# Products with h in pairs of 64 stationary columns on both column halves of the array, for two heads of one batch

## Chip, core and metric

The kernel runs on one core of a Trainium2 chip. Times are device microseconds of an execution of the whole program. TensorE multiplies: it loads a stationary tile (up to 128 rows by 128 columns) and streams a moving tile through it, with the result in PSUM. VectorE (DVE), ScalarE (ACT) and GpSimd (POOL) do the elementwise work, and SyncE (SP) issues most of the DMAs. All data are fp32.

## The reference, cut to what matters

There are two graph layers on 16 batches of 1024 nodes with 128 features, each followed by a residual sum and a layer norm. Layer 1 is the one that the change touches. Its input `X` is layer 0's output, its `A` is the adjacency, and it has four heads:

```
h      = einsum('bnf,hfd->hbnd', X, conv_w) + conv_b
scores = einsum('hbni,hij,hbmj->hbnm', h, attn_w, h)
Ah     = tanh(A * scores)
hh     = relu(einsum('hbnm,hbmd->hbnd', Ah, h))
out    = layernorm(X + relu(relu(mean over heads of hh) + X))
```

Layer 0 is an attention over the same adjacency with a masked softmax, three gates and a tanh. Of it only its place beside layer 1 matters here.

## The kernel before

Layer 1 of a batch is 32 steps: 4 heads (`hd`) by 8 blocks of 128 nodes (`m`). A step, `layer1_step(b, hd, m)`, does four things.

1. TensorE multiplies block `m` of the transposed input `x1T` with the head's `uT` (the input times the head's folded weights), in two halves `q` of 512 columns, into PSUM tiles `sc` (L704).
2. DVE multiplies each half with the adjacency into the SBUF tile `s`, 128 x 1024 (L705).
3. ACT takes the tanh of `s` in place (L706).
4. `back` multiplies `s` with the head's 128 columns of `h1` of block `m`, and adds that to the head's accumulator `acc`, 128 x 1024 in two PSUM banks (L710). The stationary operand is `h1[:, ts(hd, D)]`, 128 x 128; the moving one is a half of `s`, 128 x 512. So a step has two such products, one for each `q`, with the features of the head as output partitions and the nodes as columns. Over the 8 blocks they add up in PSUM.

After a head's eighth block, `add_head` adds the ReLU of each half of `acc` to the tile `sum` on DVE (L726 for head 0, L728 for the others). The accumulator has one buffer under its tag, so the next head's first product with h waits until both of these have read it.

The products with h are not issued in their own step. `push` puts each `back` into the queue `pending`, and with `DELAY = 2` the products of a step are issued two steps later, behind that step's score products. TensorE so has 2 steps for DVE and ACT to finish `s`.

The order of the instructions is written out by hand. Between the steps of batch b, the tables `BETWEEN` and `AHEAD` place pieces of layer 0 of batch b+1 (its products with the attention at L462, masks, softmax, gates) and of batch b+2 (its score products at L354). `head_uT` (L238) makes the next head's `uT` at a head's fifth block. There is a semaphore wait only where another engine or a DMA is to be waited for.

Another kind of TensorE product is used below for its times: in the opening, `weigh_bias` multiplies a stationary tile of only 3 rows, `rows_x` (L157), between the products at L153 and L158, whose stationary tiles are 128 x 128.

Of the kernel before, what the change touches and what calls it, by code (L numbers as in the profile page):

```python
# [24 lines left out]
def two_layer_adjacency_kernel(  # L25
# [19 lines left out]
    nc = tc.nc  # L45
    B, N, D = x.shape
    H = conv_w.shape[0]
    assert D == P and N % 512 == 0
    NB = N // P
# [144 lines left out]
    def push(back):  # L194
        pending.append(back)
        if len(pending) > DELAY:
            pending.popleft()()
# [489 lines left out]
    def layer1_step(b, hd, m):  # L687
        x1T, h1, uT = x1T_t[b], h1_t[b, m], u_t[b, hd]
        adj = adj_t[b, m]
        if m == 0:  # L690
            acc1_t[b, hd] = ps_acc.tile([P, N], F32, tag="acc1", name=f"acc1_{b}_{hd}")
        acc = acc1_t[b, hd]


        last = (b, hd) == (B - 1, H - 1)
        if last:
            if m == 0:
                kept.append(sb.tile([P, NB, N], F32, tag="R", name="kept", bufs=1))
            s = kept[0][:, m, :]
        else:  # L700
            s = sb.tile([P, N], F32, tag="s1", name=f"s1_{b}_{hd}_{m}", bufs=4)
        for q in range(NH):
            ps = ps_sc.tile([P, 512], F32, tag="sc", name=f"sc1_{b}_{hd}_{m}_{q}")
            nc.tensor.matmul(ps, x1T[:, ts(m, P)], uT[:, ts(q, 512)], start=True, stop=True)  # L704
            nc.vector.tensor_mul(s[:, ts(q, 512)], ps, adj[:, ts(q, 512)])  # L705
        nc.scalar.activation(s, s, AF.Tanh)  # L706

        def back(halves=range(NH)):
            for q in halves:
                nc.tensor.matmul(  # L710
                    acc[:, ts(q, 512)], h1[:, ts(hd, D)], s[:, ts(q, 512)],
                    start=(m == 0), stop=(m == NB - 1),
                )
            if m == NB - 1:
                if hd == 0:
                    sum_t[b] = sb.tile([P, N], F32, tag="sum", name=f"sum_{b}", bufs=1)
                for q in halves:
                    add_head(b, hd, acc[:, ts(q, 512)], q * 512)

        push(partial(back, [0]) if last else back)  # L720

    def add_head(b, hd, a, at):

        o = sum_t[b][:, at : at + a.shape[1]]
        if hd == 0:
            nc.vector.tensor_scalar_max(o, a, 0.0)  # L726
        else:
            nc.vector.scalar_tensor_tensor(o, a, 0.0, o, op0=ALU.max, op1=ALU.add)  # L728
# [142 lines left out]
    for b in range(B):  # L871
        plan = BETWEEN if b else {**BETWEEN, **FIRST}
        after = layer0(b + 2) if b + 2 < B else {}
        for step in range(H * NB):
            hd, m = divmod(step, NB)
# [81 lines left out]
```

## Time and profile before

| | |
|---|---|
| runs, device us | 2409.5, 2409.74, 2414.6; median 2409.74 |
| span of the profiled execution, first to last instruction | 2407.4 us |
| TensorE matmuls and weight loads in the profile | 5983 and 5983 |
| granted TensorE clock, mean | 0.999 of full speed |
| head 1 of batch 8, products with h | about 1299.7 to 1338.7 us of the span |
| head 2 of batch 8, products with h | about 1338.7 to 1372.8 us of the span |

The profiled execution has no time of its own besides its span; the median of the runs is 2.3 us above the span, which is what lies before the first and behind the last instruction.

The profile numbers the lines of the kernel before. "PE" is a matmul, "PEld" a weight load, which can run under a matmul. In a group's row stand the line, engine and operation, the tiles written and read, the tile of the array with its shape, and the number of instructions; then the busy time in us and the mean length of one in ns; then the engine's idle time ahead of them and what ended it. A matmul's recorded length runs from its start to its modelled end, so the lengths of two that follow each other overlap. The starts say what each costs.

### The profile page before, as it was taken

The page shows a single profiled execution, that of the slowest core. Times are in us where ns is not written, and L with a number is a line of the kernel's source. Part 1 is how long each engine was busy: PE and PEld are TensorE (multiplying, and loading weights), DVE is VectorE, ACT ScalarE, POOL GpSimd, SP SyncE. Part 2 cuts the span into 40 slices and gives each one's busy share as a digit, 9 for nine tenths or more (in the row PEclk, how much of TensorE's full clock was granted, in tenths as well). Part 3 has the DMA queues.
Part 4 walks back from the last instruction along what each step waited for, and adds up shares of the span by engine and source line. Part 5 has one row for each costly group of instructions (what it writes and reads, how often), then busy time and mean ns, then how long its engine had stood idle before and what let it go on. Part 6 is the DMA issues. An engine that isn't in the chain of part 4 may idle for free.

```text
span 2407.4 us, 20166 instructions
## 1 busy us (share of the span) xinstructions
PE 2398.8 (100%) x5983; PEld 1095.6 (46%) x5983; DVE 1551.3 (64%) x3262; ACT 1063.5 (44%) x1503; POOL 608.9 (25%) x389
## 2 busy tenths in 40 slices
PE   9999999999999999999999999999999999999999
PEld 5444444444444444444444444444444444444444
DVE  7666666766667656666666666667666576666555
ACT  6545344453444534445444454444444344443333
POOL 2214131241312313133131231313214132141000
PEclk9999999999999999999999999999999999999999
DMA  5334151442414324243242422425234252341010
GB/s 192 72 78 123 46 130 42 97 106 50 126 47 104 94 60 115 53 111 82 63 113 62 115 69 70 110 56 123 62 78 108 51 131 53 80 115 34 18 27 10
DMA packets 474194, 196.98 MB, mean 82 GB/s; under 512 B 414948, under 2 KB 440291, under 8 KB 474084
## 3 DMA queue, kind: packets, MB, share of 16 engines
q1 hardware_dynamic: 455501, 129.03, 23.0%
q0 software_dynamic: 18288, 66.59, 9.3%
q8 instruction: 48, 0.79, 0.1%
q14 instruction: 63, 0.51, 0.1%
q10 hardware_dynamic: 294, 0.07, 0.0%
HBM read 136.12 MB, written 59.51 MB: 81 GB/s over the span
## 4 chain that ended last, share of the span: by engine, by line
PE 99%; DVE 1%; ACT 0%; issue 0%; POOLq 0%; DVEq 0%
PE sc L704 36%; PE acc L710 36%; PE acc L462 9%; PE sc L354 5%; PE pR L675 5%; PE pT_u L238 5%; PE pR_h L335 1%; PE pT_q L238 1%; PE acc_other L462 0%; PE idle L136 0%; DVE R L418 0%; DVE s L705 0%; PE pt L496 0%; DVE st L214 0%; PE turn L371 0%
## 5 line engine op out<-in xcount | busy, mean ns | idle before, releaser
L705 DVE TENSOR_TENSOR s<-sc,adj 128x512 f32<-128x512 f32 x1008 | 685.1, 688 | 713.9 <-PE sc L704 692.7
L706 ACT ACTIVATE s<-s 128x1024 f32<-128x1024 f32 x504 | 533.1, 1058 | 1056.9 <-DVE s L705 897.7
L704 PE MATMUL sc<-uT,x1T 128*128 128x512 f32 x2048 | 962.8, 592 | 0.2
L710 PE MATMUL acc<-s,h 128*128 128x512 f32 x2016 | 947.3, 592 | 0.0
L710 PEld LDWEIGHTS acc<-s,h 128*128 128x128 f32 x2016 | 380.5, 190 | 484.7 <-issue 476.7
L704 PEld LDWEIGHTS sc<-uT,x1T 128*128 128x128 f32 x2048 | 386.7, 190 | 470.2 <-issue 403.5
L401 POOL TENSOR_SCALAR edge<-adj 128x1024 uint8<-128x1024 f32 x120 | 332.8, 2773 | 315.3 <-DVE top_None L418 312.9
L218 POOL TENSOR_TENSOR rs<-rs,mhalf 128x8 f32<-128x8 f32 (+3 forms) x35 | 54.2, 1549 | 881.0 <-DVE rs L217 880.9
L462 PE MATMUL acc<-R,hz 128*128 128x512 f32 x492 | 231.6, 592 | 0.2 <-ACT hz L448 0.2
L430 ACT ACTIVATE R<-R,nmax 128x1024 f32<-128x1024 f32 x126 | 144.6, 1147 | 81.0 <-DVE nmax L426 73.3
L418 DVE CUSTOM_DVE_ANT_0 R<-R,edge 128x1024 f32<-128x1024 f32 x126 | 152.8, 1213 | 0.5 <-ACT hz L448 0.5
L451 DVE TENSOR_TENSOR R<-R,adj 128x1024 f32<-128x1024 f32 (+1 forms) x127 | 152.0, 1197 | 0.0
L462 PEld LDWEIGHTS acc<-R,hz 128*128 128x128 f32 x492 | 93.1, 190 | 115.7 <-issue 111.4
L354 PE MATMUL sc<-xT,qT 128*128 128x512 f32 (+3 forms) x384 | 144.9, 486 | 0.0
L360 ACT ACTIVATE R<-sc,h 128x512 f32<-128x512 f32 (+1 forms) x192 | 111.1, 580 | 52.3 <-PE sc L354 46.8
L543 POOL TENSOR_TENSOR x1T<-hp,wu_b 128x1024 f32<-128x1024 f32 x45 | 106.4, 2363 | 103.8 <-DVE hws L549 63.6
L238 PE MATMUL pT_u<-x1T,ms 128*128 128x512 f32 x256 | 120.6, 593 | 0.0
L675 PE MATMUL pR<-cw,x1T 128*128 128x512 f32 x256 | 117.6, 598 | 0.0
L354 PEld LDWEIGHTS sc<-xT,qT 128*128 128x128 f32 x384 | 69.9, 190 | 70.0 <-issue 60.6
L302 POOL DMA_DIRECT2D adj<-in_adjT_dram x112 | 66.1, 590 | 91.8 <-DVE s L705 91.8
L728 DVE SCALAR_TENSOR_TENSOR sum<-acc,sum 128x512 f32<-128x512 f32 x95 | 61.2, 686 | 41.7 <-PE acc L710 41.7
L678 ACT COPY h<-pR 128x512 f32<-128x512 f32 x128 | 72.4, 593 | 28.2 <-PE pR L675 26.4
(163 smaller groups left out, 1151.5 us busy)
## 6 DMA issues: line engine op xcount, KB each, us to landing
adj<-in_adjT_dram POOLq DMA_DIRECT2D x112, 512.0 KB, 4.1
xT<-in_xT_dram SPq DMA_DIRECT2D x16, 512.0 KB, 4.7
adj<-in_adjT_dram SPq DMA_DIRECT2D x16, 512.0 KB, 8.8
x<-in_x_dram SPq DMA_DIRECT2D x16, 512.0 KB, 5.5
dram_hp<-turn_hp SPq DMA_DIRECT2D x15, 512.0 KB, 2.6
hp<-dram_hp SPq DMA_DIRECT2D x60, 128.0 KB, 3.1
dram_x<-turn_x SPq DMA_DIRECT2D x15, 512.0 KB, 2.9
x1T<-dram_x SPq DMA_DIRECT2D x60, 128.0 KB, 5.5
```

Source lines behind the costliest of these rows:

```text
L238: nc.tensor.matmul(ps, w, src[:, ts(q, 512)], start=True, stop=True)
L354: nc.tensor.matmul(ps[:, : at - lo], t["qT"][:, ts(j, P)], t["xT"][:, lo:at], start=True, stop=True)
L401: engine.tensor_scalar(m, adj_t[b, j], 0.0, None, ALU.is_gt)
L418: nc.vector.tensor_tensor_reduce(to[:, ks], s[:, ks], t["edge", j][:, ks], 1.0, nmax, ALU.mult, ALU.max, top)
L430: nc.scalar.activation(row(j), row(j), AF.Exp, bias=t["nmax", j], accum_out=t["z", j])
L451: nc.vector.tensor_mul(s[:, ks], s[:, ks], adj[:, ks])
L462: nc.tensor.matmul(t["acc"][q], t["hz", j], row(j)[:, ts(q, BH), :], start=(j == 0), stop=(j == NB - 1),)
L675: nc.tensor.matmul(ps, x1T_t[b][:, ts(k, P)], cw.rearrange("p h d -> p (h d)"), start=True, stop=True)
L704: nc.tensor.matmul(ps, x1T[:, ts(m, P)], uT[:, ts(q, 512)], start=True, stop=True)
L705: nc.vector.tensor_mul(s[:, ts(q, 512)], ps, adj[:, ts(q, 512)])
L706: nc.scalar.activation(s, s, AF.Tanh)
L710: nc.tensor.matmul(acc[:, ts(q, 512)], h1[:, ts(hd, D)], s[:, ts(q, 512)], start=(m == 0), stop=(m == NB - 1),)
```

## The change

In batch 8 (`B // 2`), heads 1 and 2, `back` issues four products of 64 stationary columns where it issued two of 128. `c` is the half of the head's 128 columns and `q` the half of the moving columns. Output features 0 to 63 go to PSUM partitions 0 to 63, and features 64 to 127 to partitions 64 to 127, so the first are placed on the left column half of the array and the second on the right one, as tiles of 128 rows by 64 columns. The order is in two pairs: first (`c` 0, `q` 0) with (`c` 1, `q` 1), then (`c` 0, `q` 1) with (`c` 1, `q` 0). A pair uses both column halves, with different moving data and different PSUM banks. The accumulated values are the same as before. All other batches and heads, and everything that isn't TensorE, keep their instructions.

```diff
         def back(halves=range(NH)):
-            for q in halves:
+            if b == B // 2 and hd in (1, 2):
+                for pair in (((0, 0), (1, 1)), ((0, 1), (1, 0))):
+                    for c, q in pair:
+                        nc.tensor.matmul(
+                            acc[ts(c, 64), ts(q, 512)],
+                            h1[:, hd * D + c * 64 : hd * D + (c + 1) * 64], s[:, ts(q, 512)],
+                            start=(m == 0), stop=(m == NB - 1),
+                        )
+                halves_done = ()
+            else:
+                halves_done = halves
+            for q in halves_done:
                 nc.tensor.matmul(
                     acc[:, ts(q, 512)], h1[:, ts(hd, D)], s[:, ts(q, 512)],
                     start=(m == 0), stop=(m == NB - 1),
                 )
```

The product in the new branch is at L712 of the changed kernel, the old one at L721, and the additions of `add_head` at L737 and L739.

## The prediction

> **What bounds the kernel now.** I read the page's busy times first, then the chain that ended last, then the costliest groups, and last the timeline of a product with h. The page's first part and its chain:
>
> ```profile
> PE 2398.8 (100%) x5983; PEld 1095.6 (46%) x5983; DVE 1551.3 (64%) x3262; ACT 1063.5 (44%) x1503; POOL 608.9 (25%) x389
> ```
>
> ```profile
> PE 99%; DVE 1%; ACT 0%; issue 0%; POOLq 0%; DVEq 0%
> PE sc L704 36%; PE acc L710 36%; PE acc L462 9%; PE sc L354 5%; PE pR L675 5%; PE pT_u L238 5%; PE pR_h L335 1%; PE pT_q L238 1%; PE acc_other L462 0%; PE idle L136 0%; DVE R L418 0%; DVE s L705 0%; PE pt L496 0%; DVE st L214 0%; PE turn L371 0%
> ```
>
> TensorE is the whole chain. No other engine is busy for more than 64% of the span, so whatever the change adds on TensorE goes to the end in full, and whatever it moves elsewhere is hidden. The line that changes is L710, 36% of the chain:
>
> ```profile
> L704 PE MATMUL sc<-uT,x1T 128*128 128x512 f32 x2048 | 962.8, 592 | 0.2
> L710 PE MATMUL acc<-s,h 128*128 128x512 f32 x2016 | 947.3, 592 | 0.0
> L710 PEld LDWEIGHTS acc<-s,h 128*128 128x128 f32 x2016 | 380.5, 190 | 484.7 <-issue 476.7
> ```
>
> The program has 1,016 products at L710 (504 steps of two, and the last head's 8 of one); the profile has 2,016 + 16 matmuls. So one fp32 product is two passes, each with a weight load of its own. Next the timeline at 1277 us (columns: start, length, engine, line):
>
> ```profile
> 1276.97 0.19 PEld L710 LDWEIGHTS acc<-s,h 128*128 128x128 f32 x1 [0.24 <-ACT uT L240]
> ...
> 1277.40 1.88 PE L710 MATMUL acc<-s,h 128*128 128x512 f32 x4
> 1277.40 0.19 PEld L710 LDWEIGHTS acc<-s,h 128*128 128x128 f32 x1 [0.24 <-issue]
> ...
> 1277.83 0.19 PEld L710 LDWEIGHTS acc<-s,h 128*128 128x128 f32 x1 [0.24 <-issue]
> ...
> 1278.26 0.19 PEld L710 LDWEIGHTS acc<-s,h 128*128 128x128 f32 x1 [0.24 <-issue]
> ...
> 1278.69 0.19 PEld L462 LDWEIGHTS acc<-R,hz 128*128 128x128 f32 x1 [0.24 <-issue]
> ...
> 1279.12 1.88 PE L462 MATMUL acc<-R,hz 128*128 128x512 f32 x4
> ```
>
> Passes start 0.429 us apart ((1279.12 - 1277.40) / 4 = 0.43), although each lasts 0.592: the last 0.163 us is a tail under the next pass. Every load starts at the start of the pass before its own and is over 0.24 us before it is needed. Loads are free today; a step's products cost 4 x 0.429 = 1.72 us.
>
> **What the Trainium skill says.** "TensorEngine Tiling (Array Packing)", Key Properties: tiles can load and multiply in parallel, but changing the tiling mode drains the engine. The trace has one such place, L157, whose stationary tile has 3 rows, among full-array products:
>
> ```profile
> 7.49 0.25 PE L153 MATMUL p_c<-wb_col,s_ww 128*128 128x1 f32 x1
> ...
> 7.67 0.18 PEld L157 LDWEIGHTS p_x<-ident,rows_x 3*128 3x128 f32 x1
> ...
> 7.78 0.18 PEld L157 LDWEIGHTS p_x<-ident,rows_x 3*128 3x128 f32 x1
> ...
> 7.80 0.25 PE L157 MATMUL p_x<-ident,rows_x 3*128 3x3 f32 x1
> ...
> 7.98 0.19 PEld L158 LDWEIGHTS p_x<-wb_col,a_sym 128*128 128x128 f32 x1
> ```
>
> It agrees: at both changes of form the load is not early. It starts 0.18 us after the matmul before it (7.49 to 7.67, 7.80 to 7.98), which streamed 1 and 3 columns, so nearly all of that is the tail. The next load follows 0.11 us later (7.67 to 7.78), so a load of 128 columns holds the array 0.11 us. "TensorE: Matmul & The Clock Gate", LDWEIGHTS, says that a load's time goes with its columns; for 64 I estimate half of 0.11, 0.05 us. The same page, The mechanism, says that matmuls start and end strictly in program order, and that a load overlaps a running matmul only in other rows; the trace contradicts the latter, since all L710 loads run under matmuls on the same rows. Measured speedup vs the span model gives 2.38 times for three column tiles: column tiles do run together there. No trace here has column tiles, in fp32 or otherwise.
>
> **The change part by part.** Batch 8, heads 1 and 2: 16 steps of 512. In each, two products of 128 stationary columns become four of 64, so 4 passes become 8, of 512 moving columns each. DVE, ACT, POOL and the DMA queues keep their instructions and order. I cost a step against 1.72 us.
>
> 1. Passes. If nothing overlaps: 8 x 0.429, +1.72 us. If the pairs are perfect: 4 x 0.429, +0. The order decides between them. One product's two passes use the same half of the array and come one after the other: A first, A second, B first, B second. With starts in program order, B's first pass can join A's second, but A's first finds no partner, and B's second finds one only in the next pair's first. A step of four products is then five slots, not four: first pass alone, three shared slots, last pass alone. +0.43 us.
> 2. Loads inside the chain. A load goes out when the pass before it starts, so the load for each joining pass is exposed: three times 0.05, +0.15 us. Bounds: 0 if it is pulled ahead, 3 x 0.19 = 0.57 if a whole load is waited for.
> 3. Changes of form. Every paired step lies between full-array products, so there are two per step. Going in, tail 0.18 and load 0.05; coming back, tail 0.18 and load 0.11: 0.52 us. Bounds: 0 if columns need no drain, 2 x (0.163 + 0.19) = 0.71 with whole loads.
> 4. Waits. At the ends of heads 1 and 2 the additions on DVE (L728, moved to L739) wait for the last product of the step. In the trace the first addition at 1371.27 starts after both halves' products, not after its own half's, so the pair order, which finishes both halves late, delays nothing. The next head's first product needs these additions done: they end at 1372.55 and it starts at 1372.78. The 0.23 us of slack grows by the change of form ahead of the score products between. That product also waits for the engine's own earlier matmuls, which ended over a microsecond before. Cost 0; if the cover went, 0.2 us at two places.
>
> A step: 0.43 + 0.15 + 0.52 = 1.10 us. Sixteen: 17.6 us, all on the path, since TensorE waits for nothing in these heads (39.00 of 39.00 us and 34.10 of 34.10 us busy). The span of the profile is 2407.4 us, the median of the runs 2409.7; the sum goes on the median: 2427.4 us.
>
> **The rivals.**
>
> *The halves don't run together in fp32.* Everything is in series: 1.72 + 0.52 = 2.24 us a step, 35.8 us, 2445.5. If loads too were exposed at the 7 changes of tile inside a step (7 x 0.05 x 16 = 5.6), 2451. For it: no row of the profile shows two matmuls streaming at once, and each fp32 pass already takes 0.429 us for 512 columns, so it may need paths that a second tile would want. Against it: the skill's measurement, though it names no fp32.
>
> *Pairs in lockstep.* Both halves take first passes together, then second passes: four slots, with one exposed load of 0.05 in each pair. 0.10 + 0.52 = 0.62 us a step, 9.9 us, 2419.7. It would need B to overtake A's second pass, against program order.
>
> *Not slower.* A pass over half the columns is shorter than 0.429 us. At half, 0.214, five slots are 1.07, and with loads 0.15 and changes of form 0.52 the step is 1.74 against 1.72: 0.4 us in all, 2410. In lockstep with four such slots it is 0.86 + 0.62 = 1.48, -3.8 us, 2406. It decides once five slots fall to 0.21 us each. Against it: passes in the profile cost by moving columns (0.59 for 512, 0.28 for 132), and the change moves no fewer per pass.
>
> **How the numbers follow.** Chain of five slots 0.47 (2419 to 2434, with item 2 or item 3 at its bounds), series 0.36 (2437 with free changes of form, 2451 with exposed loads), lockstep 0.10, not slower 0.07. About what a measurement of this kernel can tell is 0.2%, 4.8 us. Lockstep and the two ahead of it are slower by more than that; of the last 0.07, 0.05 lands within it and 0.02 below. Faster 0.02, same 0.05, slower 0.93. The prediction is the chain's 2427.5 us; the range leaves out no loss and half of the lockstep below, and the worst of the series above: 2415 to 2450.
>
> **What would show it.** In the changed profile the paired matmuls are 128 passes with a 128*64 form. In the chain case B's first pass starts about 0.05 us after A's second, and so on in close twos; in series all eight starts are 0.43 apart. Each paired step is preceded and followed by a load that starts about 0.6 us after the last full pass's start, not with it. Other engines' busy times stay. The forecast is wrong if eight starts are evenly spaced, if no load is late at the change of form, or if steps outside the 16 move.

## The result, and the profile after

The changed kernel takes 2414.82 us (median of 18 runs), the one before 2409.54 (18 runs): ratio 1.0021, 95% interval 1.0014 to 1.0027. It is slower by 5.3 us, 0.33 us for each of the 16 steps; 17.6 us were forecast. Nearly all executions of every kernel here, the one before too, fall into two groups 5.2 to 5.4 us apart (2409.5 and 2414.7 before, 2414.8 and 2420.2 after); a time below is the median, which lies in the lower group, or the lower group's time where a kernel has only four runs.

The page after, busy times and the chain that ended last:

```profile
PE 2403.9 (100%) x6047; PEld 1089.6 (45%) x6047; DVE 1552.4 (64%) x3262; ACT 1063.0 (44%) x1503; POOL 608.4 (25%) x389
```

```profile
PE 97%; DMA 1%; DVE 1%; SPq 0%; ACT 0%; issue 0%; POOLq 0%; DVEq 0%
```

TensorE still is the path; the 1% of DMA lies in the opening, before 36 us. Its 64 more matmuls add 5.1 us busy; the span grows by 5.4 (2407.4 to 2412.8), and the other engines' busy times stay within about 1 us of what they were. The costliest groups:

```profile
L704 PE MATMUL sc<-uT,x1T 128*128 128x512 f32 x2048 | 963.2, 592 | 0.2
L721 PE MATMUL acc<-s,h 128*128 128x512 f32 x1952 | 917.2, 592 | 0.0
...
L721 PEld LDWEIGHTS acc<-s,h 128*128 128x128 f32 x1952 | 368.5, 190 | 469.3 <-issue 461.7
```

The 64 passes that L710 lost are 128 at L712 now. The instructions that write `acc` between 1299 and 1380 us (length in ns as shortest, median and longest):

```profile
L712 PEld LDWEIGHTS acc<-s,h x128: 132/136/137, 1299.5 to 1375.3; 128*64 128x64 f32 x128
L712 PE MATMUL acc<-s,h x128: 592/592/643, 1299.5 to 1375.7; 128*64 128x512 f32 x128
L462 PEld LDWEIGHTS acc<-R,hz x8: 186/190/190, 1301.4 to 1307.9; 128*128 128x128 f32 x8
L462 PE MATMUL acc<-R,hz x8: 592/592/697, 1301.4 to 1308.3; 128*128 128x512 f32 x8
```

Then the first paired step on the timeline, matmuls first, then weight loads:

```profile
1299.00 0.59 PE L704 MATMUL sc<-uT,x1T 128*128 128x512 f32 x1
...
1299.53 1.94 PE L712 MATMUL acc<-s,h 128*64 128x512 f32 x8
1301.39 1.12 PE L462 MATMUL acc<-R,hz 128*128 128x512 f32 x2
...
1299.53 0.20 PEld L712 LDWEIGHTS acc<-s,h 128*64 128x64 f32 x4 [0.76 <-issue]
1300.01 0.14 PEld L712 LDWEIGHTS acc<-s,h 128*64 128x64 f32 x2 [0.29 <-issue]
1300.44 0.14 PEld L712 LDWEIGHTS acc<-s,h 128*64 128x64 f32 x2 [0.28 <-issue]
1301.39 0.30 PEld L462 LDWEIGHTS acc<-R,hz 128*128 128x128 f32 x2 [0.81 <-issue]
```

Eight passes of 592 to 643 ns lie within 1.94 us: four slots and a tail, where a slot is the 0.43 us from one full pass's start to the next. They start in twos, at 0.522 and 0.529 us after the last score pass's start, then 1.002 and 1.009, 1.432 and 1.438, 1.861 and 1.867. The loads are in twos as well. This is lockstep: the second column half adds 0.006 us a step.

The loss stands at the two changes of form, from full-array products to column tiles and back. Without one, the next pass would start 0.429 us after the last score pass (1299.00); the first load waits until 0.52, so **0.09 us**, which I call the drain. The first paired pass then waits for its load, which makes its record 643 ns long instead of 592: **0.05 us**. On the way out the last two passes start at 1.861 and 1.867 and fill their slot until 2.296; the next load starts at 2.39, again 0.09 late, and the first pass at L462 is 697 ns long, 0.11 more than 592. Sum: 0.09 + 0.05 + 0.01 + 0.09 + 0.11 = 0.35 us. From the last score pass to the second pass behind the products it is 2.923 us in every step that has a full-length pass there, against 6 x 0.429 = 2.574 with full products: 0.349. In all 16 steps the loss so counted is the same to 1 or 2 ns, so they are 5.6 us, against 5.3 between the medians. The last full pass ahead of the first paired step starts 0.28 us earlier in this trace than in the one before (1299.00 against 1299.29), after the same instructions, so at the end of the stretch these two traces, too, are 5.3 us apart.

### The profile page after: what moved, and what is told of

Its sections match the earlier page's. It is cut to its first block, busy times and chain, and to the rows that moved or that the text cites. A ratio compares the mean times of both kernels' runs of the same rounds, so it can differ in the third digit from the quotient of the medians.

```text
span 2412.8 us, 20295 instructions
## 1 busy us (share of the span) xinstructions
PE 2403.9 (100%) x6047; PEld 1089.6 (45%) x6047; DVE 1552.4 (64%) x3262; ACT 1063.0 (44%) x1503; POOL 608.4 (25%) x389
## 4 chain that ended last, share of the span: by engine, by line
PE 97%; DMA 1%; DVE 1%; SPq 0%; ACT 0%; issue 0%; POOLq 0%; DVEq 0%
PE sc L704 36%; PE acc L721 35%; PE acc L462 9%; PE sc L354 5%; PE pT_u L238 5%; PE pR L675 5%; PE acc L712 1%; PE pR_h L335 1%; PE pT_q L238 1%; DMA adj<-in_adjT_dram 1%; DMA cw_in<-in_L_gnn_conv_w_dram 0%; SPq L302 0%; SPq L268 0%; DMA R<-dram_turn 0%; PE acc_other L462 0%
## 5 line engine op out<-in xcount | busy, mean ns | idle before, releaser
L721 PE MATMUL acc<-s,h 128*128 128x512 f32 x1952 | 917.2, 592 | 0.0
L721 PEld LDWEIGHTS acc<-s,h 128*128 128x128 f32 x1952 | 368.5, 190 | 469.3 <-issue 461.7
L462 PE MATMUL acc<-R,hz 128*128 128x512 f32 x492 | 231.8, 593 | 0.2 <-ACT hz L448 0.2
L462 PEld LDWEIGHTS acc<-R,hz 128*128 128x128 f32 x492 | 92.9, 190 | 116.4 <-issue 112.3
L739 DVE SCALAR_TENSOR_TENSOR sum<-acc,sum 128x512 f32<-128x512 f32 x95 | 61.3, 686 | 42.7 <-PE acc L721 40.2
```

What stands on the lines that cost most here:

```text
L462: nc.tensor.matmul(t["acc"][q], t["hz", j], row(j)[:, ts(q, BH), :], start=(j == 0), stop=(j == NB - 1),)
L721: nc.tensor.matmul(acc[:, ts(q, 512)], h1[:, ts(hd, D)], s[:, ts(q, 512)], start=(m == 0), stop=(m == NB - 1),)
```

## The experiments

Why do the halves run together, although in the program a left product's second pass stands ahead of the right product's first? And is all of the loss at the changes of form? The diffs below are cut, and show the paired branch of `back` against the changed kernel where nothing else is said; `...` stands for lines left out.

**Left products first, then right.**

```diff
-                for pair in (((0, 0), (1, 1)), ((0, 1), (1, 0))):
-                    for c, q in pair:
+                for c, q in ((0, 0), (0, 1), (1, 0), (1, 1)):
```

> The four products of a step stand as left, left, right, right instead of left, right, left, right. Theory 'own queue': each column half takes its passes in order but independently of the other half, so the right half starts with the left one though four left passes stand ahead of it; four slots of 0.43 us a step, the time of the changed kernel, about 2414.8 us (5.3 over before). Rival 'neighbours only': a pass of one half can overtake just the pass next to it; here the right half's first pass comes to run beside the left half's fourth, seven slots, 3 x 0.43 x 16 = 20.6 us more, about 2435. Rival 'both passes of one product run side by side': the left products then take two slots and the right ones two, again about 2414.8, and the next experiment tells it apart.

Measured: 2415.13 us, ratio 1.0022 (1.0015 to 1.0028), as the changed kernel. The timeline of its first paired step:

```profile
1299.33 0.59 PE L704 MATMUL sc<-uT,x1T 128*128 128x512 f32 x1
1299.86 0.66 PE L711 MATMUL acc<-s,h 128*64 128x512 f32 x2
...
1299.86 1.94 PE L711 MATMUL acc<-s,h 128*64 128x512 f32 x8
```

The first two rows show what runs in a stretch of 10 ns at 1299.88: the end of a score pass, and two passes of the products with h. The third row is the whole step, eight passes in four slots. If passes of one half stay in series, which the next experiment tests, the second of the two is the right half's first, and it starts with the left one though four left passes stand ahead of it; only the lag goes from 0.006 to 0.013 us. The seven slots of "neighbours only" are out.

**All on the left half.**

```diff
-                for pair in (((0, 0), (1, 1)), ((0, 1), (1, 0))):
-                    for c, q in pair:
+                for c, q in ((0, 0), (1, 1), (0, 1), (1, 0)):
+                    to = 0 if 0 < m < NB - 1 else c
...
-                            acc[ts(c, 64), ts(q, 512)],
+                        acc[ts(to, 64), ts(q, 512)],
```

The order of the four products stays; only the half that they go to changes.

> For the inner six blocks of both heads (12 of the 16 steps) all four products of 64 columns go to the left column half, so the right half idles; features 64 to 127 of these two heads are left out of the result and features 0 to 63 get a wrong sum. Theories 'own queue' and 'neighbours only' both say that passes on one half can't overlap: eight slots in place of four, 12 x 4 x 0.43 = 20.6 us over the changed kernel, about 2435.4. Rival 'both passes of one product run side by side': no change, about 2414.8.

Measured: 2435.5 us, 20.7 over the changed kernel's; over all four runs the ratio to before is 1.0113 (1.0098 to 1.0127). A step's matmuls, and what runs in a stretch of 10 ns at 1310.70:

```profile
1310.61 3.65 PE L712 MATMUL acc<-s,h 128*64 128x512 f32 x8
1314.19 1.12 PE L462 MATMUL acc<-R,hz 128*128 128x512 f32 x2
...
1310.61 0.64 PE L712 MATMUL acc<-s,h 128*64 128x512 f32 x1
```

Eight passes take 3.65 us on one half, one at a time, whether two neighbours belong to one product or to two. So neither the two passes of one product nor two products on one half run side by side. What ran side by side in the changed kernel must be passes of different halves: the right half's first pass overtakes the left one's second.

**Two steps' products together.**

```diff
-                for pair in (((0, 0), (1, 1)), ((0, 1), (1, 0))):
-                    for c, q in pair:
+                joined.append((h1, s, m))
+                if m % 2 == 0:
+                    return
+                for c, q, (h1_, s_, m_) in [(c, q, j) for j in joined for c, q in ((0, 0), (1, 1), (0, 1), (1, 0))]:
...
+                joined.clear()
```

The products take `h1_`, `s_` and `m_` of their own step.

> The paired products of two steps are issued together, at the second of them: 8 changes of form in and 8 out, where there were 16 and 16. Theory 'the loss is all at the change of form' (0.35 us a step in the trace: at the way in 0.09 drain and 0.05 load, at the way out 0.09 and 0.11): 8 x 0.35 = 2.8 us less than the changed kernel, about 2412.0, 2.5 over before. Rival 'the loss goes with the paired passes or with something else in these steps': about 2414.8. A score buffer or an s buffer that comes free too late would add to either, and show as idle time of TensorE.

Measured: 2412.04 us, 2.6 over before (2409.40 in this comparison); ratio 1.0006 (0.9998 to 1.0014).

```profile
1302.51 0.59 PE L704 MATMUL sc<-uT,x1T 128*128 128x512 f32 x1
...
1303.03 3.65 PE L714 MATMUL acc<-s,h 128*64 128x512 f32 x16
1306.62 0.70 PE L462 MATMUL acc<-R,hz 128*128 128x512 f32 x1
```

Sixteen passes take eight slots with one way in and one way out. The interval alone does not exclude that nothing was lost, but the trace shows the loss of one step, once for two: from the score pass to the pass at L462 it is 4.11 us, 0.25 more than nine slots, and that pass is 0.11 us longer than 0.59. The paired work is the same, half of the changes are gone, and with them half of the loss.

**The same moving half in a pair.**

```diff
-                for pair in (((0, 0), (1, 1)), ((0, 1), (1, 0))):
-                    for c, q in pair:
+                for c, q in ((0, 0), (1, 0), (0, 1), (1, 1)):
```

> The products of a pair stream the same half of s and write the same PSUM bank, in different partitions: (0,0) with (1,0), then (0,1) with (1,1). Theory 'own queue': only the column half decides, so about 2414.8 us as the changed kernel. Rival 'the halves run together only with different banks or different moving data': eight slots, 16 x 4 x 0.43 = 27.5 us more, about 2442.

Measured: 2414.82 us, ratio 1.0020 (1.0012 to 1.0028). Eight slots would be 27.5 us more, so the passes still run in pairs: different moving halves and banks are not needed for it here.

**Two steps together, all left products first.** Against two steps joined:

```diff
-                for c, q, (h1_, s_, m_) in [(c, q, j) for j in joined for c, q in ((0, 0), (1, 1), (0, 1), (1, 0))]:
+                for c, q, (h1_, s_, m_) in [(c, q, j) for c in range(2) for j in joined for q in range(2)]:
```

> As with two steps joined, but all four left products of the two steps stand ahead of all four right ones: eight left passes must be overtaken. Theory 'own queue' with room for eight passes and their loads: as the joined kernel, about 2412.0 us, with the right half's start a few ns later for every product that stands ahead of it. Rival 'room for four passes only' (the most that the kernel with left then right has shown): the right half starts when the left one has four passes to go, twelve slots in place of eight, 8 x 4 x 0.43 = 13.7 us more, about 2426.

Measured: 2426.19 us, 14.2 over the joined kernel; ratio 1.0076 (1.0063 to 1.0088). The rival with room for four holds. The whole of two joined steps, and what runs in stretches of 0.1 us or less at 1303.5, 1305.03 and 1307.0:

```profile
1303.25 5.42 PE L714 MATMUL acc<-s,h 128*64 128x512 f32 x16
...
1303.25 0.64 PE L714 MATMUL acc<-s,h 128*64 128x512 f32 x1
...
1304.59 1.08 PE L714 MATMUL acc<-s,h 128*64 128x512 f32 x3
...
1306.80 0.59 PE L714 MATMUL acc<-s,h 128*64 128x512 f32 x1
```

First one pass at a time, then twos, then one at a time again. The third row is the left half's fourth and fifth passes and the right half's first, which starts 2.296 us after the last score pass's start, just after the left half's fifth (2.290), when three left ones are still to come. So overtaking has a limit: a pass came past one running and three waiting passes; while the left half's fourth pass ran, with four waiting, it did not. That makes twelve slots: 8 x 4 x 0.43 = 13.7 us. From the second shared slot on the right passes start 0.057 us behind the left ones, since the right half's first pass waited for its load as at a way in (0.05 us); 8 x 0.057 = 0.5 us more.

**Quarters of 32 columns.**

```diff
-                for pair in (((0, 0), (1, 1)), ((0, 1), (1, 0))):
-                    for c, q in pair:
+                for turn_ in range(NH):
+                    for c in range(4):
+                        q = (c + turn_) % 2
-                            acc[ts(c, 64), ts(q, 512)],
-                            h1[:, hd * D + c * 64 : hd * D + (c + 1) * 64], s[:, ts(q, 512)],
+                            acc[ts(c, 32), ts(q, 512)],
+                            h1[:, hd * D + c * 32 : hd * D + (c + 1) * 32], s[:, ts(q, 512)],
```

> Each product in tiles of 32 stationary columns, eight products a step: quarters 0 to 3 with the first four (neighbours on different halves of s), then quarters 0 to 3 again with the other halves. Theory 'every column strip has its own queue': again four slots a step, sixteen passes in fours; loads of 32 columns make the way in 0.03 us shorter, and the fourth quarter starts some 0.02 us late; about 2414.8 us. Rival 'two halves at once and no more' (only so many streams can be fed): eight slots, 27.5 us more, about 2442.

Measured: 2414.93 us, ratio 1.0029 (1.0018 to 1.0040): as the halves. A step's matmuls, and what runs in a stretch of 20 ns at 1299.68:

```profile
1299.65 1.92 PE L713 MATMUL acc<-s,h 128*32 128x512 f32 x16
...
1299.65 0.64 PE L713 MATMUL acc<-s,h 128*32 128x512 f32 x4
```

Four passes are under way at once, and sixteen fill four slots.

**The scores in pairs too.** In the 16 steps that issue paired products (`sc_q` holds the step's two score tiles):

```diff
+        paired, sc_q = b == B // 2 and 10 <= hd * NB + m < 26, []
...
+        if paired:
+            for c, q in ((0, 0), (1, 1), (0, 1), (1, 0)):
+                nc.tensor.matmul(
+                    sc_q[q][ts(c, 64)], x1T[:, m * P + c * 64 : m * P + (c + 1) * 64],
+                    uT[:, ts(q, 512)], start=True, stop=True,
+                )
+            for q in range(NH):
+                nc.vector.tensor_mul(s[:, ts(q, 512)], sc_q[q], adj[:, ts(q, 512)])
```

> The score products of the same 16 steps, just ahead of the paired products with h, are in pairs of 64 columns too. Twice as many paired passes, but 26 changes of form in place of 32, since three steps now follow each other with no full product between. Theory 'the loss is all at the change of form': 6 x 0.17 = 1.0 us less than the changed kernel, about 2413.8. Rival 'each paired step loses by its passes': 16 more paired sets, 5.3 us more, about 2420. DVE starts its product with the adjacency up to 0.9 us later in these steps, since both halves of the scores end together; that should be hidden.

Measured: 2413.99 us, 4.6 over before; ratio 1.0015 (1.0006 to 1.0024). Twice the paired passes didn't cost more, where the rival has 10.6 us: the loss doesn't go with them.

**Every head.**

```diff
-            if b == B // 2 and hd in (1, 2):
+            if not last:
```

> The change in every head but the last one of the last batch: 504 steps in place of 16, 1,008 changes of form. Theory 'the loss is all at the change of form', 0.33 to 0.35 us a step: 504 x 0.33 = 166 to 504 x 0.35 = 176 us over before, 2576 to 2586 us. Rival 'the loss has a part that comes once' (a wait at the first or last paired head): clearly less than 166; rival 'paired steps bring other engines late in the fuller stretches': more than 176, with idle time of TensorE by its waits for DVE or ACT.

Measured: 2582.2 us, 172.8 over before; over all four runs the ratio is 1.0731 (1.0717 to 1.0746). That is 0.343 us a step, and TensorE waits for nothing new (its waits on other engines sum to 2.9 us in the whole span, 2.8 before). All in a row:

| kernel | changes of form in and out of paired products | us over before | us for one |
|---|---|---|---|
| two steps together | 16 | 2.6 | 0.165 |
| scores in pairs too | 26 | 4.6 | 0.177 |
| the change | 32 | 5.3 | 0.165 |
| every head | 1,008 | 172.8 | 0.171 |
| trace of the change, mean of in and out | | | 0.174 |

## Why the prediction was wrong

The bound was right: TensorE is the path, what was added on it arrived at the end, and the other engines stayed as they were. The sign was right too, for the reason given: the drain at each change of form was the right kind of cost. The size was too high by 12.3 us (17.6 against 5.3), and 2414.82 lies just under the range. Every term that was off was too high, so none made up for another. By its steps:

1. **Passes, +0.43 us a step: this step failed.** It said five slots because starts come in program order, and called lockstep a case against that order. Measured are four slots, +0. All-on-left shows that one half alone gives eight slots, and with that left-then-right shows passes of one half overtaken by the other's. The order argument holds within one column half only. The Trainium skill's "TensorE: Matmul & The Clock Gate", The mechanism, on which I leaned, says that matmuls keep strict program order; across column tiles these runs differ, and decide. This step alone is 6.9 us.
2. **Loads inside the chain, +0.15.** Measured 0.006. It fell with step 1: in lockstep both halves' next loads run under the passes, as full loads did before; only the loads at the way in are exposed, and step 3 counts them. 2.3 us.
3. **Changes of form, +0.52.** The mechanism was right: what the Trainium skill's "TensorEngine Tiling (Array Packing)", Key Properties, says of a drain at a change of tiling mode agrees with this trace, where the load is 0.09 us late at each change. Measured 0.34. The loads came out as forecast (51 and 105 ns); the drain was mis-sized, 0.09 instead of 0.18. I read it from a matmul of 1 and one of 3 moving columns, start to next load, and took all of it for tail. From passes of 512 columns, what comes after the 0.429 us slot is 0.09; what makes up the other 0.09 behind the short matmuls, no run tried. The tail of 0.163 us in a record, which the upper bound took, isn't what the change of form waits for either: the load at 1299.53 starts ahead of the score pass's recorded end at 1299.59. 2.9 us.
4. **Waits at the heads' ends, 0.** Right: the steps around the ends of heads 1 and 2 lose the same 0.35 us as all others, and every head in pairs brought no wait.

The three terms sum to 6.9 + 2.3 + 2.9 = 12.1 of the 12.3 us. The lockstep rival had 0.62 us a step for a measured 0.33; with the right drain, and without the loads that it still counted inside the pairs, it would have been 0.34. I gave it one chance in ten, because I set a statement on order, which nothing in the trace of before could show for column tiles, above the skill's other one, that column tiles run together.

No version here beats the kernel before. A pair of halves does in four slots what two full products do in four, so the changes of form are pure loss; joining steps only makes them fewer.

## What to carry to other kernels

Splitting a product that fills the array into column tiles gained nothing here and cost a drain and an exposed load at each change of form, 0.17 us, so group products of one form. Tiles of 64 or 32 stationary columns on different column strips ran side by side in fp32 at next to no cost of their own (here they were cut from an operand of 128; one that really has so few columns wasn't tried), provided that they alternate closely in program order: eight passes of one half ahead of the other's already lost the overlap for half of them. Read the cost of a drain from a long pass, as next load minus start minus slot, not from a one-column one.

## What the runs showed that I had not expected

- Matmuls on different column tiles overtake each other: past one running and three waiting passes, and not past one running and four waiting. What sets that limit, and whether the loads count in it, wasn't tried.
- Both passes of an fp32 product on one column half stay in series (3.65 us for eight); four strips of 32 columns run at once, with starts 0.007 us apart.
- The exposed part of a weight load goes with its columns: the first passes' extra length was 25 ns for 32 columns (617 ns against 592), 51 for 64 and 105 for 128.
